# Gate and up of two feed-forward batches by 49 block products in place of 56, and the feed-forward input by way of DRAM

## The chip, the cores and the metric

The kernel runs on one core of one Trainium2 chip. A core has a matrix engine (TensorE, PE in the profile; its weight loads are shown apart as PEld), a vector engine (DVE), a scalar engine (ACT), GpSimd (POOL) and SyncE (SP), which here only issues transfers. Each engine works through its own instructions in their order; semaphores hold one back until another is done. Matrix products write to PSUM (eight banks of 128 x 512 fp32 values), all else lies in SBUF or in DRAM. The metric is the device time of one execution in microseconds, the median of several runs.

## The reference, cut to what matters

Four batches of 512 tokens with 512 channels go through an attention block of the gated delta rule and a gated feed-forward, each with a modulated layer norm in front and a gate behind. What the change touches is the feed-forward:

```python
def _L0_ffn_ref(x, w_gate, w_up, w_down):
    gate = jnp.einsum('bsd,hd->bsh', x, w_gate)
    up = jnp.einsum('bsd,hd->bsh', x, w_up)
    gated = jax.nn.silu(gate) * up
    return jnp.einsum('bsh,dh->bsd', gated, w_down)
...
h = _layernorm(x, axis=-1) * (1 + cb) + sb
x = x + gb * _L0_ffn_ref(h, L0_ffn_w_gate, L0_ffn_w_up, L0_ffn_w_down)
```

Here s is 512, d is 512 and h is 2048; all is fp32.

## The kernel before

The kernel is written with tile pools, and a scheduler of the framework sets the order on each engine: it takes the program's order as a priority and moves instructions forward where it expects an engine to be free. So work of a later stage fills gaps in an earlier one. The stages stand in this order: projections and convolutions of batch 0, its delta rule, projections of the others, and then feed-forward and delta rule in turn: `triangles(2)`, `feed_forward(0)`, `delta_rule(2)`, `triangles(3)`, `feed_forward(1)`, `delta_rule(3)`, `feed_forward(2)`, `feed_forward(3)`.

`delta_rule(b)` goes through four chunks of 128 tokens. `operands` (L609) prepares, `scan` (L682) is the sequential part (products pf at L695 and pm at L704 with copies between them, eight steps per batch), `finish` and `project` normalise, multiply by the output weights (pwo, L745) and write the residual `xmid` to DRAM, and `turned` (L759) transposes the normed result (pxn, L762) into the SBUF tile `hf[b]`, of four channel blocks by 512 tokens. `pending` holds steps that the next scan steps pop.

`feed_forward(b)` takes `hf[b]` and goes over the 16 hidden blocks of 128 in pairs (`for i in range(0, NF, 2)`). For each pair `two_blocks` makes gate and then up: a product of 2 x 2 blocks by Strassen's scheme in Winograd's form, seven products of 256 x 256 x 256 in place of eight. Each of them is two fp32 matrix products 128 x 128 by 128 x 256. The sums of the weights were made once, early, by `weight_sums` and lie in DRAM as `wsum` (seven blocks for each pair); the sums of the input (`hs`, L833 to L836) are made once per batch. The results are added up by ACT copies and DVE additions from PSUM (L965 to L974). Silu (L989) and the product of gate and up (L990) finish a hidden tile `hid`.

Four hidden blocks are a quarter. Down works by quarters: `down` as plain products (pd, L847, 128 x 512, 16 of them), with a multiplication by the gate on DVE (L852) and an addition on POOL (L853); or `down_by_seven` (pds, L890, 28 products 128 x 256), with POOL sums of the hidden tile (L865 to L868), weight sums from DRAM (`dsum`, made by POOL in `feed_forward(1)`, L1004 to L1007) and an accumulator in SBUF (ACT L892, DVE L894). By seven go quarters 1 to 3 of batch 2 and 0 to 2 of batch 3; `seven_to_output` turns the accumulator into output in six steps that `some` hands out between products.

PSUM has three banks for `fill` (products of projections and feed-forward), three for `seq` (the delta rule) and two as `scratch`.

Of the kernel before, what the change touches and what calls it, by code (L numbers as in the profile page):

```python
# [33 lines left out]
LATER = 4000  # L34


@with_exitstack
def adaln_block(
# [29 lines left out]
    w1 = ctx.enter_context(tc.tile_pool(name="w1", bufs=1))  # L68
    stage_b = ExitStack()
# [25 lines left out]
    kd, qd, vd, sd, gd, xmid = ([] for _ in range(6))  # L95
    for b in range(B):
        kd.append(dr.tile([P, NP, T], F32, name=f"kd{b}"))
        qd.append(dr.tile([P, NP, T], F32, name=f"qd{b}"))
        vd.append(dr.tile([NT, P, H, DV], F32, name=f"vd{b}"))
        sd.append(dr.tile([NT, DV, H, P], F32, name=f"sd{b}"))  # L100
        gd.append(dr.tile([2, 2, H, NT, C + 1], F32, name=f"gd{b}"))
        xmid.append(dr.tile([T, D], F32, name=f"xmid{b}"))
    wsum = [dr.tile([NF // 2, P, 7, 2, P], F32, name=f"wsum{i}") for i in range(2)]
# [109 lines left out]
    def load_x(b):  # L213
        ts = []
        if b == 2:

            room = w1.tile([P, NT, D], F32, tag="hf", bufs=2, name=f"xt{b}")
        for c in range(NT):
            if b == 2:
                t = room[:, c, :]  # L220
            else:
                t = pa_.tile([P, D], F32, tag="xt", bufs=4, name=f"xt{b}_{c}")
            (act if b else sp).dma_start(t, x[b, c * P : (c + 1) * P, :])
            ts.append(t)
        return ts
# [298 lines left out]
    ex, at, td, ttd, hf = {}, {}, {}, {}, {}  # L524

    def triangles(b):
# [9 lines left out]
        kp = w1.tile([P, NP, T], F32, tag="kp", bufs=1, name=f"kp{b}")  # L536
# [50 lines left out]
        pm = w1.tile([n, S, S], F32, tag="pm", name=f"pm_{b}")  # L587
        sp.dma_start(pm, ad)
        t = w1.tile([n, S, S], F32, tag="ti", name=f"ti_{b}")
        tmp = w1.tile([n, S * S // 4], F32, tag="tip", name=f"tip_{b}")  # L590
# [168 lines left out]
    def turned(b, c, xn):  # L759
        pt = seq(f"pxn{b}_{c}")  # L760
        for k in range(KD):
            pe.transpose(pt[:, k * P : (k + 1) * P], xn[:, k * P : (k + 1) * P], ident)  # L762
        for k in range(KD):
            act.activation(
                hf[b][:, k, c * P : (c + 1) * P], pt[:, k * P : (k + 1) * P], AF.Identity,
                bias=mod_t[:, 2, k, b : b + 1], scale=mod_t[:, 3, k, b : b + 1],
            )

    def delta_rule(b):
        ga = w1.tile([P, D], F32, tag="ga", name=f"ga{b}")  # L770
        sp.dma_start(ga, gate_d[0, b].partition_broadcast(P))
        hf[b] = w1.tile([P, KD, T], F32, tag="hf", bufs=2, name=f"hf{b}")
        st = operands(b, 0)
        for c in range(NT):
            nxt = operands(b, c + 1) if c + 1 < NT else None
            o = scan(b, c, st, nxt)
            finish(b, c, o, ga)
            st = nxt
# [35 lines left out]
    def feed_forward(b):  # L814
        nonlocal pd_

        own = pd_ if b == B - 1 else pc_
        gb = own.tile([P, D], F32, tag="gb", bufs=1, name=f"gb{b}")
        sp.dma_start(gb, gate_d[1, b].partition_broadcast(P))
        xm = []  # L820
        for c in range(NT):
            t = own.tile([P, D], F32, tag="xm", bufs=NT, name=f"xm{b}_{c}")
            sp.dma_start(t, xmid[b][c * P : (c + 1) * P, :])
            xm.append(t)
        ht = hf[b]
# [4 lines left out]
        if more is None:  # L830
            more = own.tile([P, 3, 2, TH], F32, tag="hs", bufs=1, name=f"hs{b}")
# [6 lines left out]
        tdn, acc, left = {}, {}, {}  # L838

        fast = {2: [1, 2, 3], 3: [0, 1, 2]}.get(b, [])  # L840
# [15 lines left out]

        def left_factors(q, j):

            hid = hids[q, j]
            a11, a12, a21, a22 = (  # L860
                hid[:, k, i * TH : (i + 1) * TH] for i in range(2) for k in range(2)
            )
            t = pd_.tile([P, 3, TH], F32, tag="sd", bufs=4, name=f"sd{b}_{q}_{j}")
            s1, s2, s4 = (t[:, k] for k in range(3))
            pool.tensor_add(s1, a21, a22)  # L865
            pool.tensor_sub(s2, s1, a11)
            pool.tensor_sub(a21, a11, a21)
            pool.tensor_sub(s4, a12, s2)  # L868
            left[q, j] = a11, a12, a22, a21, s1, s2, s4

        def down_by_seven(q):


            sums = {}
            for j in range(2):
                a11, a12, a22, a21, s1, s2, s4 = left[q, j]
                wd = wdn[q, j].rearrange("p j (h d) -> p j h d", h=2)
                d1, d2, d4, d3 = (tdn[q, j][:, k] for k in range(4))
                sums[j] = [
                    (a11, wd[:, 0, 0]), (a12, wd[:, 1, 0]), (s2, d2), (s1, d1), (a21, d3),  # L880
                    (s4, wd[:, 1, 1]), (a22, d4),
                ]
            if q == fast[0]:
                acc[0] = pd_.tile([P, 7, 2, 2 * P], F32, tag="acc", bufs=1, name=f"acc{b}")
            for k in range(7):
                o = fill(f"pds{b}_{q}_{k}").rearrange("p (c d) -> p c d", c=2)
                for c in range(2):
                    for j in range(2):
                        l, r = sums[j][k]
                        pe.matmul(o[:, c], l[:, c * P : (c + 1) * P], r, start=j == 0, stop=j == 1)  # L890
                if q == fast[0]:
                    act.copy(acc[0][:, k], o)  # L892
                else:
                    vec.tensor_add(acc[0][:, k], o, acc[0][:, k])  # L894

        def quarter(q):
            if q not in fast:
                return down(q)
            down_by_seven(q)
            if q == fast[-1]:  # L900
                ending.append(seven_to_output())

        def seven_to_output():

            p1, p2, p6, p5, p7, p3, p4 = (acc[0][:, k] for k in range(7))

            def add_to(tokens, k, v):
                ds = slice(k * TH, (k + 1) * TH)
                vec.tensor_tensor(v, v, gb[:, None, ds].broadcast_to([P, 2, TH]), ALU.mult)
                for c in range(2):  # L910
                    pool.tensor_add(xm[tokens + c][:, ds], xm[tokens + c][:, ds], v[:, c])

            vec.tensor_add(p6, p6, p1)
            vec.tensor_add(p1, p1, p2)
            yield
            vec.tensor_add(p7, p7, p6)
            add_to(0, 0, p1)
            yield
            vec.tensor_add(p2, p6, p5)
            vec.tensor_add(p2, p2, p3)  # L920
            yield
            vec.tensor_add(p4, p4, p7)
            add_to(0, 1, p2)
            yield
            vec.tensor_add(p5, p5, p7)
            add_to(2, 0, p4)
            yield
            add_to(2, 1, p5)
            if fast[-1] == NQ - 1:
                for i in range(NT):  # L930
                    sp.dma_start(out[b, i * P : (i + 1) * P, :], xm[i])

        def some(n):
            while ending and n:
                n -= 1
                if next(ending[0], 1):
                    ending.clear()
# [9 lines left out]
        def two_blocks(o, n, src, i):  # L947
# [6 lines left out]
            def product(l, r):  # L954
                count[0] += 1
                if count[0] % 2 == 0:
                    some(1)
                o = half(n)
                for k in range(2):
                    pe.matmul(o, l[:, k], r[:, k], start=k == 0, stop=k == 1)  # L960
                return o
# [14 lines left out]
        for i in range(0, NF, 2):  # L976
# [3 lines left out]
            wd = own.tile([P, 2, D], F32, tag="fwd", bufs=2, name=f"wdn{b}_{i}")  # L980
# [11 lines left out]
            if i == (0 if b == B - 1 else 2):  # L992
                complete()
                if b == 2:
                    stage_b.close()
                    pd_ = ctx.enter_context(
                        tc.tile_pool(name="pd", bufs=2, side="right", reuse_waits="tile")
                    )
            if b == 1:
# [9 lines left out]
            if q in fast:  # L1009
                tdn[q, j] = pd_.tile([P, 4, 2 * P], F32, tag="td", bufs=4, name=f"td{b}_{q}_{j}")  # L1010
                sp.dma_start(tdn[q, j], dsum[i // 2])
                left_factors(q, j)
            if j == 0 and q > 0:
                quarter(q - 1)
        if b == 2:
            pending.append(lambda: quarter(NQ - 1))
        else:
            some(9)
            quarter(NQ - 1)


    pd_ = None
    ending, count = [], [0]
# [38 lines left out]
    pc_ = ctx.enter_context(tc.tile_pool(name="pc", bufs=2, reuse_waits="tile"))  # L1062
# [11 lines left out]
    feed_forward(2)  # L1074
    feed_forward(3)
# [45 lines left out]
```

## Time and profile before

| | us |
|---|---|
| median of 3 runs | 1312.97 (1311.42 to 1314.52) |
| profiled execution, first to last instruction | 1315.2 |
| stretch of the feed-forward of batches 2 and 3 (after the last transposes of batch 3) | from 1043.3 on |
| one quarter in that stretch (1058.86 to 1095.84) | 36.98 |

The profiled execution gives no time but its span, which is 2.2 us above the median of the runs. A row of the profile's groups has the source line, engine, operation, tiles (written from read), form and count; then the busy time and the mean duration of one in ns; then how long the engine was idle just before them and who ended that. An fp32 matrix product shows as two PE records, each with a weight load. In the chain that ended last each piece has its start, its length and the number of instructions.

### The profile page before, as it was taken

To read this page: it belongs to the slowest core of one execution; us is meant where nothing else is said; L and a number is where in the kernel's file an instruction comes from. 1 tells how busy PE (TensorE), PEld (TensorE's weight loads), DVE (VectorE), ACT (ScalarE), POOL (GpSimd) and SP (SyncE) were. 2 spreads that over 40 slices of the span, in tenths; PEclk is the share of its full clock that TensorE was granted. 3 is DMA by queue.
4 is the path that set the end of the run, shared out by engine and by line. 5 is a ranking of instruction groups with operands and counts; after the bars stand their busy time and mean duration, and the time that the engine had idled before them with its cause. 6 is when DMAs were issued, how large, how long until landed. Compare 5 with 4: busy or idle time off the path is not lost.

```text
span 1315.2 us, 18413 instructions
## 1 busy us (share of the span) xinstructions
PE 1234.9 (94%) x6752; PEld 807.1 (61%) x6752; DVE 733.7 (56%) x1574; ACT 383.5 (29%) x740; POOL 290.8 (22%) x357
## 2 busy tenths in 40 slices
PE   6799898999889998999999999799999999999998
PEld 3345355554344565767757666666666578888884
DVE  3665865656188255784445558543555543563564
ACT  2633355554142354211103332101134312112110
POOL 4100214533210012030023121233111221131113
PEclk9799898999899999999999999899999999999999
DMA  7579667667874537664436555544632555444431
GB/s 209 138 203 288 186 173 209 172 212 249 255 205 126 144 98 176 199 202 139 134 113 189 124 126 165 161 130 150 193 85 70 174 186 175 146 152 152 140 114 62
DMA packets 217945, 214.57 MB, mean 163 GB/s; under 512 B 95608, under 2 KB 164216, under 8 KB 217856
## 3 DMA queue, kind: packets, MB, share of 16 engines
q1 hardware_dynamic: 194976, 176.58, 46.4%
q10 hardware_dynamic: 19360, 17.93, 4.2%
q0 software_dynamic: 3520, 18.89, 3.8%
q8 instruction: 54, 0.88, 0.3%
q14 instruction: 35, 0.29, 0.1%
HBM read 159.23 MB, written 50.97 MB: 160 GB/s over the span
## 4 chain that ended last, share of the span: by engine, by line
PE 64%; DVE 14%; DMA 11%; POOL 5%; issue 3%; ACT 2%; SPq 1%; POOLq 0%; DVEq 0%; ACTq 0%
PE phg L960 14%; PE phu L960 11%; PE pd L847 9%; PE pwo L745 5%; PE pds L890 4%; PE pp_v L424 3%; PE pp_g L424 3%; PE pm L704 2%; DVE ti L602 2%; PE scratch L631 2%; DMA wsum<-wsg 2%; DVE tip L598 2%; DMA wsum<-wsu 2%; PE pp_q L424 1%; PE pp_k L424 1%
## 5 line engine op out<-in xcount | busy, mean ns | idle before, releaser
L847 PE MATMUL pd<-wdn,hid 128*128 128x512 f32 x320 | 140.6, 592 | 0.0
L960 PE MATMUL phg<-hf,wg 128*128 128x256 f32 x512 | 138.4, 387 | 1.8 <-DMA wg<-wsum 1.8
L960 PE MATMUL phg<-hs,wg 128*128 128x256 f32 x384 | 103.6, 390 | 5.9 <-DVE hid L967 5.8
L960 PEld LDWEIGHTS phg<-hf,wg 128*128 128x128 f32 x512 | 95.9, 192 | 20.7 <-issue 6.3
L960 PE MATMUL phu<-hf,wu 128*128 128x256 f32 x384 | 101.1, 388 | 2.2 <-DMA wu<-wsum 2.0
L847 PEld LDWEIGHTS pd<-wdn,hid 128*128 128x128 f32 x320 | 60.7, 190 | 68.1 <-issue 63.6
L960 PE MATMUL phu<-hs,wu 128*128 128x256 f32 x384 | 95.6, 382 | 2.5 <-DVE up L973 2.5
L424 PE MATMUL pp_g<-ht,wg 128*128 128x512 f32 x192 | 91.6, 617 | 5.7 <-DMA wg<-in_w_g_dram 4.6
L853 POOL TENSOR_TENSOR xm<-xm,tmpf 128x512 f32<-128x512 f32 x40 | 50.9, 1273 | 206.8 <-DVE tmpf L852 206.8
L424 PE MATMUL pp_v<-ht,wv 128*128 128x512 f32 x192 | 89.3, 609 | 3.5 <-DVE v L503 2.3
L745 PE MATMUL pwo<-wo,ot 128*128 128x512 f32 x192 | 91.8, 608 | 0.0
L965 ACT COPY hid<-phg 128x256 f32<-128x256 f32 x32 | 11.9, 372 | 247.9 <-PE phg L960 247.9
L960 PEld LDWEIGHTS phg<-hs,wg 128*128 128x128 f32 x384 | 71.5, 193 | 20.4 <-DVE hid L967 8.3
L960 PEld LDWEIGHTS phu<-hs,wu 128*128 128x128 f32 x384 | 71.9, 191 | 19.2 <-DVE up L973 7.1
L960 PEld LDWEIGHTS phu<-hf,wu 128*128 128x128 f32 x384 | 71.7, 192 | 15.5 <-issue 3.1
L424 PEld LDWEIGHTS pp_g<-ht,wg 128*128 128x128 f32 x192 | 35.1, 195 | 43.0 <-issue 41.8
L852 DVE TENSOR_TENSOR tmpf<-pd,gb 128x512 f32<-128x512 f32 x40 | 27.5, 689 | 59.4 <-PE pd L847 44.7
L424 PEld LDWEIGHTS pp_v<-ht,wv 128*128 128x128 f32 x192 | 35.2, 193 | 41.5 <-issue 38.5
L989 ACT ACTIVATE hid<-hid 128x1024 f32<-128x1024 f32 x32 | 33.8, 1057 | 86.2 <-DVE hid L973 70.0
L434 DVE SCALAR_TENSOR_TENSOR acc_v<-pp_v,conv_v,acc_v 128x511 f32<-128x511 f32 (+2 forms) x72 | 53.4, 743 | 9.8 <-ACT acc_v L432 8.8
L704 PE MATMUL pm<-r,l 128*128 128x128 f32 x384 | 53.8, 285 | 1.0 <-ACT r L700 0.9
L704 PEld LDWEIGHTS pm<-r,l 128*128 128x128 f32 x384 | 48.2, 194 | 8.9 <-ACT r L700 4.7
(244 smaller groups left out, 2060.1 us busy)
## 6 DMA issues: line engine op xcount, KB each, us to landing
wdn<-in_w_down_t_dram SPq DMA_DIRECT2D x32, 512.0 KB, 4.3
wg<-wsum SPq DMA_DIRECT2D x32, 512.0 KB, 3.8
wu<-wsum SPq DMA_DIRECT2D x32, 512.0 KB, 3.6
wg<-wsum SPq DMA_DIRECT2D x32, 384.0 KB, 4.4
wu<-wsum SPq DMA_DIRECT2D x32, 384.0 KB, 4.3
wsum<-wsg POOLq DMA_DIRECT2D x8, 896.0 KB, 4.3
wsum<-wsu POOLq DMA_DIRECT2D x8, 896.0 KB, 4.6
vd<-v SPq DMA_DIRECT2D x24, 256.0 KB, 3.4
```

What stands on the lines that cost most here:

```text
L424: pe.matmul(pp, w[:, k, :], ht[:, k, :], start=(k == 0), stop=(k == KD - 1))
L434: vec.scalar_tensor_tensor(acc[:, i:], pp[:, : T - i], taps[:, col, TAPS - 1 - i : TAPS - i], acc[:, i:], ALU.mult, ALU.add,)
L598: vec.tensor_tensor(v, pm[:, j, j + 1 :, None].broadcast_to([n, m, j]), t[:, j : j + 1, :j].broadcast_to([n, m, j]), ALU.mult,)
L602: vec.tensor_add(t[:, j + 1 :, :j], t[:, j + 1 :, :j], v)
L704: pe.matmul(pm[:, h], l[:, hs.start + h, 2 * par : 2 * par + 2, :], r[:, par, hs.start + h], start=True, stop=True,)
L745: pe.matmul(pw, ot[:, h, :], wo[:, h, :], start=(h == 0), stop=(h == H - 1))
L847: pe.matmul(pd, hids[q, i // 2][:, i % 2, c * P : (c + 1) * P], wdn[q, i // 2][:, i % 2, :], start=(i == 0), stop=(i == NQ - 1),)
L852: vec.tensor_mul(tmp, pd, gb)
L853: pool.tensor_add(xm[c], xm[c], tmp)
L890: pe.matmul(o[:, c], l[:, c * P : (c + 1) * P], r, start=j == 0, stop=j == 1)
L960: pe.matmul(o, l[:, k], r[:, k], start=k == 0, stop=k == 1)
L989: act.activation(hid, hid, AF.Silu)
```

## The change

The feed-forward input goes through DRAM in all batches. `turned` writes each chunk's transposed result to `hd[b]`, and `feed_forward` (now of batches 0 and 1 alone) loads it into a tile of its own. `kp`, `pm`, `ti`, `tip` of `triangles` move to a pool that is closed before the last two batches, and their feed-forward starts with a new pool `pe`. `dsum` is made in `feed_forward(0)`.

Batches 2 and 3 are computed by a new function `tail`. Gate and up of a quarter (four hidden blocks, four channel blocks, four token blocks of 128) are one `two_level` call: the 2 x 2 scheme of seven products, and each of the seven again by seven, so 49 products of 128 x 128 x 128 in place of 56 (28 products of 128 x 128 x 256). The outer weight sums come from `wsum` as before; the inner ones are made by POOL for each call. A call goes in two halves, of 4 and of 3 outer products: each inner product is a group of 4 or 3 matrix products into one bank. Three banks serve a half: partial sums are left in PSUM, the next group is added to them there, and ACT or DVE takes out the values on the way. The last group of a half (`ending_`) is deferred into the next half, with the DVE additions that unite the outer level. The input sums for both levels are made once per batch (`moving`). Down goes by seven in all quarters but the last of batch 3; `some` is called once per half.

```diff
+TAIL = 2
...
-            room = w1.tile([P, NT, D], F32, tag="hf", bufs=2, name=f"xt{b}")
+            room = pa_.tile([P, NT, D], F32, tag="xr", bufs=1, name=f"xt{b}")
...
+        h = w1.tile([P, KD, P], F32, tag="hf", bufs=2, name=f"hf{b}_{c}")
         for k in range(KD):
             act.activation(
-                hf[b][:, k, c * P : (c + 1) * P], pt[:, k * P : (k + 1) * P], AF.Identity,
+                h[:, k, :], pt[:, k * P : (k + 1) * P], AF.Identity,
                 bias=mod_t[:, 2, k, b : b + 1], scale=mod_t[:, 3, k, b : b + 1],
             )
+        sp.dma_start(hd[b][:, :, c * P : (c + 1) * P], h)
...
-        ht = hf[b]
+        ht = pc_.tile([P, KD, T], F32, tag="hf", bufs=1, name=f"ht{b}")
+        sp.dma_start(ht, hd[b])
...
-            if b == 1:
+            if b == 0:
...
+    def differences(y11, y12, y21, y22, t1, t2, t4):
+        vec.tensor_sub(t1, y12, y11)
+        vec.tensor_sub(t2, y22, t1)
+        vec.tensor_sub(y12, y22, y12)
+        vec.tensor_sub(t4, y21, t2)
+
+    def moving(own, b):
+        y = own.tile([P, 7, 4, P], F32, tag="y", bufs=1, name=f"y{b}")
+        z = own.tile([P, 3, 7, P], F32, tag="z", bufs=1, name=f"z{b}")
+        for m, i, j in ((0, 0, 0), (1, 1, 0), (4, 0, 1), (5, 1, 1)):
+            sp.dma_start(
+                y[:, m].rearrange("p (k t) x -> p k (t x)", k=2),
+                hd[b][:, 2 * i : 2 * i + 2, j * TH : (j + 1) * TH],
+            )
+        differences(y[:, 0], y[:, 4], y[:, 1], y[:, 5], y[:, 3], y[:, 2], y[:, 6])
+        for ms in (slice(0, 4), slice(4, 7)):
+            differences(*(y[:, ms, j] for j in range(4)), *(z[:, j, ms] for j in range(3)))
+        return y, z
+
+    def two_level(o, n, src, q, yz, then):
+        y, z = yz
+        for s, m0, nm in ((0, 0, 4), (1, 4, 3)):
+            ms = slice(m0, m0 + nm)
+            nn = f"{n}_{s}"
+            w = pc_.tile([P, 2, 4, 2, P], F32, tag="fw", bufs=2, name=f"w{nn}")[:, :, :nm]
+            e = pc_.tile([P, 3, 4, P], F32, tag="fe", bufs=2, name=f"e{nn}")[:, :, :nm]
+            for a in range(2):
+                sp.dma_start(w[:, a], src[2 * q + a][:, ms])
+            x11, x12, x21, x22 = (w[:, a, :, k] for a in range(2) for k in range(2))
+            s1, s2, s4 = (e[:, j] for j in range(3))
+            pool.tensor_add(s1, x21, x22)          # L968
+            pool.tensor_sub(s2, s1, x11)           # L969
+            pool.tensor_sub(x21, x11, x21)         # L970
+            pool.tensor_sub(s4, x12, s2)           # L971
...
+            products(ba, x11, y11, True)
+            act.copy(p1, ba)
+            products(bb, s1, t1, True)
+            act.copy(p5, bb)
+            settle()
+            some(1)
+            products(ba, s2, t2, False)
+            act.copy(u2, ba)
+            bc = view(seq(f"pc{nn}"))
+            products(bc, x12, y21, True)
+            vec.tensor_add(c11, bc, p1)            # L1006
+            products(bb, s4, y22, False)
+            vec.tensor_add(c12, bb, u2)            # L1008
+            products(ba, x21, t3, False)
+            vec.tensor_add(c22, ba, p5)            # L1010
+
+            def ending_(...):
+                products(ba, x22, t4, False)
+                act.copy(c21, ba)
+                v = [o[:, :, j] for j in range(4)]
+                if s == 0:
+                    vec.tensor_add(v[1], v[1], v[0])   # L1017
+                    vec.tensor_add(v[2], v[2], v[0])
+                    vec.tensor_add(v[0], v[2], v[3])
+                else:
+                    r = [part[:, :, j] for j in range(3)]
+                    vec.tensor_add(v[2], v[2], r[0])   # L1022
+                    vec.tensor_add(v[3], v[3], v[2])
+                    vec.tensor_add(v[0], v[0], r[1])
+                    vec.tensor_add(v[2], v[2], r[2])   # L1025
+                    then()
+            left_over.append(ending_)
...
+    def tail(bs):
...
+                h = quarter_of(b, q, yz)           # gate: two_level, then Silu over 128x2048
...
+                if late:
+                    late()                         # down of the quarter before
...
+                two_level(
+                    u, f"u{b}_{q}", wsum[1], q, yz,
+                    lambda u=flat[0], h=flat[1]: vec.tensor_mul(u, u, h),   # L1069, 128x2048
+                )
...
+    def down_of(b, q, u, held, ends):              # by seven (L1135), the last quarter plain (L1100)
...
     delta_rule(3)
-    feed_forward(2)
-    feed_forward(3)
+    stage_c.close()
+    stage_t.close()
+    pc_ = ctx.enter_context(tc.tile_pool(name="pe", bufs=2, reuse_waits="tile"))
+    tail(list(range(TAIL, B)))
```

`products(bank_, l, r, first)` issues one matrix product per outer block (L991), the first with `start` set where `first` is true.

## The prediction

> **What bounds the kernel now.** I read the page's busy table first, then the chain that ended last, then the stretch of the last two batches in windows, then single rows. The first lines say that the matrix engine is the kernel:
>
> ```profile
> span 1315.2 us, 18413 instructions
> PE 1234.9 (94%) x6752; PEld 807.1 (61%) x6752; DVE 733.7 (56%) x1574; ACT 383.5 (29%) x740; POOL 290.8 (22%) x357
> ```
>
> The windows cut out two quarters (four hidden blocks of gate and up, plus one down product by seven) of batch 2. PE is busy over 99% of them at the full clock; DVE and POOL are far from it:
>
> ```profile
> core 0: us, PE busy (x) PEld busy (x) DVE busy (x) ACT busy (x) POOL busy (x), PEclk, DMA share, GB/s
> 1058.86:1095.84 36.98, 36.85 (x170) 31.46 (x169) 15.00 (x31) 9.67 (x17) 7.17 (x9) 1.00 0.40 132
> 1095.84:1132.80 36.96, 36.72 (x169) 31.45 (x169) 18.33 (x36) 5.46 (x11) 5.93 (x8) 1.00 0.48 158
> ```
>
> The chain in order of time gives the price of one record (each fp32 product is two records). Its pieces have no gap in them:
>
> ```profile
> 1049.85 9.01 PE pd L847 x21
> 1058.86 6.04 PE phg L960 x28
> ...
> 1085.91 9.93 PE pds L890 x46
> ```
>
> So 6.04/28 = 0.2157 us for 128x256, 9.93/46 = 0.2159 for the same width in the down products, 9.01/21 = 0.429 for 128x512. A quarter's sum is 112 x 0.2157 + 56 x 0.2159 = 36.25 us against 36.97 measured: 0.7 us of waiting. Saving PE work therefore saves time, as long as nothing else becomes late. Rows for the rest (groups by form; the last column of the POOL and ACT rows is idle time, not cost):
>
> ```profile
> L704 PE MATMUL pm<-r,l 128*128 128x128 f32 x384 | 53.8, 285 | 1.0 <-ACT r L700 0.9
> L853 POOL TENSOR_TENSOR xm<-xm,tmpf 128x512 f32<-128x512 f32 x40 | 50.9, 1273 | 206.8 <-DVE tmpf L852 206.8
> L990 DVE TENSOR_TENSOR hid<-hid,up 128x1024 f32<-128x1024 f32 x32 | 39.9, 1248 | 0.4
> L852 DVE TENSOR_TENSOR tmpf<-pd,gb 128x512 f32<-128x512 f32 x40 | 27.5, 689 | 59.4 <-PE pd L847 44.7 <-POOL xm L853 14.7
> L892 ACT COPY acc<-pds 128x512 f32<-128x512 f32 x14 | 8.2, 586 | 21.6 <-PE pds L890 21.6
> ```
>
> **Step A, the streams: -20.1 us.** Gate and up of two batches are 32 calls of 28 records now: 896 x 0.2157 = 193.3 us. After, 16 calls of 98 records at 128x128 = 1568. In the trace, L704 records (128x128, each with its own weights) start 0.1115 us apart at the median (quartiles 0.111 and 0.112): 174.8 us, 18.5 less. A block product has an eighth less work, but at half the width a record costs 0.517 of the wide one, so 3.4% of these streams is given back. Also one more down product goes by seven: 32 x 0.429 = 13.7 against 56 x 0.2159 = 12.1, 1.6 less. Bounds: no cost at the borders of groups, as in the x28 piece above, is what I take; at worst each of the 7 groups in 32 halves pays one 51 ns semaphore record that PE's sequencer shows in the L960 answer: 224 x 0.051 = +11 us.
>
> **Step B, the new cover: +3.4 us in each of 7 places, +23.5 us.** Today PE reads weight sums that were made once. Now each half (4 or 3 block columns) needs four POOL sums, three or four PSUM evictions by ACT, three by DVE, and then three or four DVE adds over 128x512 (L1017 to L1025), and a DVE product of 128x2048 ends each quarter. By the rows: POOL per quarter 2 x (4 x 1.27 + 4 x 1.0) + 4 x 1.27 = 23 us; DVE 2 x (3 x 0.69 + 3 x 0.53 + 7 x 0.69) + 2.4 + 7 x 0.69 = 24 us; PE 2 x 98 x 0.1115 + 12.1 = 33.9 us. On average all fits under PE, so I walk through the place where it need not: up of one quarter followed directly by gate of the next, in the order in which the changed program's instructions stand on each engine. Time 0 is the first product of up; before it a down product has let both weight buffers and their sums get ready.
> - Up's 46 products in front of gate's first end at 46 x 0.223 + 0.15 = 10.4 (0.15 for the ACT copy of the first bank: 0.29 + 0.09 + 0.59 against 0.89 us of cover).
> - Gate's first weights: the buffer (two deep) is free when the deferred product of up's first half ends at 7.9; a 256 KB load lands after 2.8 us (xr), the second of the pair at about 3.7 (512 KB, wg): 10.9 and 11.7. PE waits 0.45, runs to 11.8.
> - Up's deferred product stands next and needs the DVE sum L1010, which stands behind L1017, L1018, L1006, L1019, L1008 on DVE; the first of these waits for ACT until 8.6. 8.6 + 3 x 0.69 + 2 x 0.53 + 0.53 and gaps = 12.4: PE waits 0.65.
> - Gate's fifth group needs POOL's fourth sum: 11.8 + 4 x 1.27 = 16.9, and PE is there at 15.8: 1.2.
> - Now DVE does four adds and the 128x2048 product for up before it may take gate's sums. Clean they end at 14.05 + 4 x 0.7 + 2.4 = 19.3. But POOL is working then, and DVE rows with both inputs in SBUF grow under it: L909 (128x512) 0.675 alone and 0.875 under POOL, L971 (128x256) 0.43 and 0.87, while L970 with a PSUM input stays at 0.425. I take the 128x512 row, x 1.3: 20.9. The down product in PE's order waits for it (0.7), and the next gate bank is freed two DVE sums later, 22.3, where PE without waits would be at 18.8.
> - The last deferred product again stands behind DVE: 0 to 1.2, taken 0.6.
>
> Together 4.1 us against today's 0.7: +3.4. Bounds: DVE clean leaves 0.45 + 0.65 + 1.2 + 0.1 = 2.4 (+1.7); with x 2 on the adds and x 1.75 on the product (L990's longest is 2.15 us) 6.0 (+5.3). Seven such places (quarters 1 to 3 of batch 2, all four of batch 3): +23.5, from +12 to +37. A gain here is excluded: 0.7 is all there is.
>
> [...]
>
> **Step C, the end: +4.5 us.** The last up quarter is one tile: the copy 0.09 + 0.47, four adds 2.8, product 2.4 and gaps are 6 us in which PE has nothing, then 32 x 0.429 = 13.7 as today. Today the last wait is split: PE stands about 1.5 us between 1283 and 1299 (16.0 less 14.97 busy, and modelled ends). Bounds +2 and +6.
>
> **Step D, the first feed-forward: +4 us.** Its input goes to DRAM and back, 1 MB and four DVE subtractions later, and the changed PE order has no gate product any more in front of the last transposes of batch 1's delta rule (11 products, 22 x 0.2157 = 4.7 us, stand there now, and the profile shows them between 521.99 and 535.2 in waits for POOL and DVE). Bounds 0 and 4.7. For the second feed-forward the load hides under down of the first (13.7 us).
>
> **Step E, the delta rule of batch 3: +3 us.** Batch 2's gate starts after y and z are loaded and built (12 DVE instructions, about 7.7 us), so the PE order puts the last down of batch 1 there and has no foreign product between the second and fourth step of the scan. Foreign work from the first scan step to the last transposes falls from 28.7 to 26.4 us. Batch 1 did this stretch with 20.4 us of it in 95.0 us, batch 3 with 28.7 in 97.2: below some 25 us PE waits for the scan. Bounds 0 and 8. The moved dsum sums (32 x 0.73 us of POOL) go from one feed-forward to another of the same length; POOL idles there three quarters of the time: nothing. The SP queue gets four more stores and loads per batch, all behind work that lands long before: nothing; were an output store to hold up a weight load at the change of batch, 2 us.
>
> **Sum.** -20.1 + 23.5 + 4.5 + 4 + 3 = +14.9 us on the span of 1315.2: 1330.1. The median of the runs is 1312.97, 2.2 under this span, so 1328.
>
> **The rivals.** *Faster.* The four adds and the 2048 product end before PE needs the bank (DVE alone at them, as the rows without POOL show), and only the load and the POOL sum are waited for. Then a place costs 1.2 us, +0.5: -20.1 + 3.5 + 11.5 = -5, 1308. It decides at 1.9 us of waiting per place: below that the change gains. For it speaks DVE's 24 us under 33.9; against it that POOL works 23 of the same 34 us. 17%. *DVE becomes the bound.* If every SBUF-only instruction doubles (12 us per quarter), DVE needs 36 of 33.9 us and each quarter is 36 plus today's 0.7 and the load: 6 to 8 us per place, +45 on average: 1313 + 45 - 20.1 + 11.5 = 1349. 15%. *Narrow records don't hold 0.1115 in short groups:* step A's +11 on top, 1339. 8%. *Everything meets at nothing:* 4%. My forecast of a slower kernel near 1328: 56%.
>
> **How the numbers follow.** The range: low end from B's and C's lower bounds with D and E at 1 us each, -20.1 + 12 + 2 + 2 = -4, widened to the faster rival's lower half, 1304; high end from B's upper bound with the others as taken, -20.1 + 37 + 11.5 = +28, and on towards the DVE rival, 1347. What a measurement can tell from no change is about 0.2%, 2.6 us. Faster by more: 17%, the faster rival less its near misses, plus the tail of the main case. Within: 6%. Slower: 77%.
>
> **What would show it.** Right: a changed profile with L991 records 0.11 us apart inside a group, some 175 us in all; quarters of 37 to 39 us instead of 33.9, with PE waits put down to DVE L1008, L1010 and L1069 and POOL L971; L1017 to L1025 at 0.8 to 1.0 us mean; a hole of 5 to 6 us in front of L1100. Wrong: quarters of 35 us or less, L1069 at 2.4 us, or PE waits that name DMA alone.

## The result, and the profile after

Slower, as forecast, but by 101.6 us and not by 15: 1415.36 us at the median (1411.40 to 1416.23, four runs) against 1313.74 (1311.42 to 1316.38) for the kernel before, a ratio of 1.0766, interval 1.0743 to 1.0789. The forecast was 1328, its range ended at 1347. The profiled execution took 1411.40 us with a span of 1409.7, 94.5 more than the span before.

The head of the page:

```profile
span 1409.7 us, 20205 instructions
PE 1248.8 (89%) x7448; PEld 844.1 (60%) x7448; DVE 843.3 (60%) x1569; ACT 426.8 (30%) x796; POOL 473.2 (34%) x461
```

PE falls from 94% to 89%. DVE has five instructions less and 110 us more of busy time: its instructions have become longer. Two quarters of the tail in windows, cut from one 128x2048 product (L1069) to the next:

```profile
core 0: us, PE busy (x) PEld busy (x) DVE busy (x) ACT busy (x) POOL busy (x), PEclk, DMA share, GB/s
1119.40:1163.20 43.80, 38.74 (x254) 35.71 (x253) 30.36 (x34) 10.36 (x17) 28.42 (x21) 0.93 0.39 133
1163.20:1206.80 43.60, 37.40 (x256) 34.38 (x255) 31.38 (x34) 10.36 (x17) 28.61 (x21) 0.97 0.38 133
```

A quarter takes 43.6 us where it took 36.97 before and where its products alone need 33.9. Neither DVE (31) nor POOL (29) is full. The groups of the tail point to why (busy, mean ns; then idle before):

```profile
L1069 DVE TENSOR_TENSOR up<-up,hid 128x2048 f32<-128x2048 f32 x8 | 23.6, 2952 | 0.3
L969 POOL TENSOR_TENSOR eg<-eg,wg 128x384 f32<-128x384 f32 x7 | 16.7, 2381 | 0.5
L1024 DVE TENSOR_TENSOR hid<-hid,partg 128x512 f32<-128x512 f32 x7 | 12.3, 1752 | 0.0
L971 POOL TENSOR_TENSOR eg<-wg,eg 128x512 f32<-128x512 f32 x7 | 12.0, 1707 | 0.0
```

L1024 has the size of L852's 0.69 us and takes 1.75; L971 has the size of L853's 1.27 and takes 1.71; L969, over 128x384 (1.00 us at its shortest in this run), takes 2.4. PE's longest waits in the tail, and the hole before the last down product:

```profile
PE pbg L991 <- POOL eg L971: 15.4, 8, 2.2
PE pds L1135 <- ACT acc L1137: 8.5, 2, 6.8
PE pag L991 <- DMA wg<-wsum: 7.8, 6, 2.7
PE pag L991 <- DVE partg L1010: 7.3, 6, 1.5
PE pd L1100 <- issue: 5.6, 1, 5.6
```

Now the two engines side by side in one change from up to gate (timelines of DVE and of POOL; start, us):

```profile
1157.47 0.70 DVE L1022 TENSOR_TENSOR up<-up,partu 128x512 f32<-128x512 f32 x1 [2.06 <-ACT partu L1014]
1158.10 1.75 DVE L1024 TENSOR_TENSOR up<-up,partu 128x512 f32<-128x512 f32 x1
1159.77 1.75 DVE L1023 TENSOR_TENSOR up<-up 128x512 f32<-128x512 f32 x1
1161.56 1.63 DVE L1025 TENSOR_TENSOR up<-up,partu 128x512 f32<-128x512 f32 x1
1163.22 2.97 DVE L1069 TENSOR_TENSOR up<-up,hid 128x2048 f32<-128x2048 f32 x1
```

```profile
1157.70 1.60 POOL L969 TENSOR_TENSOR eg<-eg,wg 128x512 f32<-128x512 f32 x1
1159.26 1.72 POOL L970 TENSOR_TENSOR wg<-wg 128x512 f32<-128x512 f32 x1
1160.94 1.71 POOL L971 TENSOR_TENSOR eg<-wg,eg 128x512 f32<-128x512 f32 x1
1162.61 1.44 POOL L968 TENSOR_TENSOR eg<-wg 128x384 f32<-128x384 f32 x1
1164.13 2.93 POOL L969 TENSOR_TENSOR eg<-eg,wg 128x384 f32<-128x384 f32 x1
```

Start plus length gives the ends: L1024 ends 0.55 us after sum L969, sum L970 1.13 us after L1024, L1023 0.54 after L970, and so on. They take turns, one add and one sum every 1.67 us. The last sum begins inside the product and ends 0.87 us after it. Only the first add, which begins as a sum ends, takes its 0.70.

**Where the 94.5 us are.** For each stretch I take the records on PE times their start-to-start median (0.112 us for 128x128, 0.216 for 128x256, 0.429 for 128x512, the small shapes likewise); what is left of the stretch I call waiting. The streams of the whole program fall from 1034.9 to 1015.3 us (-19.6). Waiting before the first scan step goes from 71.6 to 67.3 us (-4.3; in the runs below the first scan step comes at 172 to 179 us, with the change and without, so this is no part of it). From there to the end of the last delta rule it goes from 195.6 to 227.0 (+31.4), in the tail behind it from 13.1 to 100.0 (+86.9). The sum is +94.4.

Some 14 of the tail's 100.0 us are not waiting but slower records. In eight stretches of 3.4 or 6.8 us between 1094 and 1391 us the granted clock is 0.50, and records start 0.213 us (128x128) and 0.427 us (128x256) apart in them. They come upon waits of 6.80, 1.96, 1.96, 1.97, 1.96, 1.96, 2.42 and 5.60 us; behind four others, of 2.18, 2.94, 2.71 and 1.96 us, it stays at 1.00. The tail of the kernel before has no such stretch while products run. One of them beside an undisturbed group of the same size (PE's timeline, then the window):

```profile
1157.68 1.16 PE L991 MATMUL pbg<-z,eg 128*128 128x128 f32 x8
1162.70 2.07 PE L991 MATMUL pbg<-y,eg 128*128 128x128 f32 x8 [1.96 <-POOL eg L971]
```

```profile
core 0: us, PE busy (x), PEclk, DMA share, GB/s
1162.60:1166.00 3.40, 3.30 (x15) 0.50 0.02 5
```

### The profile page after: what moved, and what is told of

Same layout as the page of the kernel before. It is cut to its first block, busy times and chain, and to the rows that moved or that the text cites. A ratio compares the mean times of both kernels' runs of the same rounds, so it can differ in the third digit from the quotient of the medians.

```text
span 1409.7 us, 20205 instructions
## 1 busy us (share of the span) xinstructions
PE 1248.8 (89%) x7448; PEld 844.1 (60%) x7448; DVE 843.3 (60%) x1569; ACT 426.8 (30%) x796; POOL 473.2 (34%) x461
## 4 chain that ended last, share of the span: by engine, by line
PE 53%; DVE 19%; DMA 11%; POOL 8%; issue 5%; ACT 2%; SPq 2%; POOLq 0%; ACTq 0%; DVEq 0%
PE pd L848 7%; PE phg L876 6%; PE phu L876 5%; PE pwo L749 4%; PE pp_v L428 3%; DMA wg<-wsum 3%; PE pp_g L428 2%; PE pag L991 2%; PE pau L991 2%; PE pm L708 2%; PE scratch L635 2%; PE pds L1135 2%; DVE ti L606 2%; DVE tip L602 2%; DMA wsum<-wsu 2%
## 5 line engine op out<-in xcount | busy, mean ns | idle before, releaser
L848 PE MATMUL pd<-wdn,hid 128*128 128x512 f32 x256 | 115.3, 597 | 0.0
L848 PEld LDWEIGHTS pd<-wdn,hid 128*128 128x128 f32 x256 | 47.6, 190 | 50.5 <-issue 48.2
L876 PE MATMUL phg<-ht,wg 128*128 128x256 f32 x256 | 72.0, 400 | 3.8 <-DVE yk L646 2.0
L730 POOL TENSOR_TENSOR osq<-o 128x768 f32<-128x768 f32 x16 | 23.7, 1483 | 108.2 <-ACT o L716 108.2
L438 DVE SCALAR_TENSOR_TENSOR acc_v<-pp_v,conv_v,acc_v 128x509 f32<-128x509 f32 (+2 forms) x72 | 53.3, 743 | 10.8 <-ACT acc_v L436 9.9
L876 PEld LDWEIGHTS phg<-ht,wg 128*128 128x128 f32 x256 | 49.6, 199 | 16.0 <-issue 3.3
L876 PE MATMUL phg<-hs,wg 128*128 128x256 f32 x192 | 52.8, 395 | 6.1 <-DVE hid L883 5.8
L749 PEld LDWEIGHTS pwo<-wo,ot 128*128 128x128 f32 x192 | 35.0, 198 | 32.2 <-issue 29.4
L853 DVE TENSOR_TENSOR tmpf<-pd,gb 128x512 f32<-128x512 f32 x32 | 22.0, 689 | 49.4 <-PE pd L848 46.7
L428 PE MATMUL pp_q<-ht,wq 128*128 128x512 f32 x96 | 51.4, 671 | 0.0
L876 PE MATMUL phu<-ht,wu 128*128 128x256 f32 x192 | 49.1, 381 | 0.4 <-DMA wu<-wsum 0.4
L428 PE MATMUL pp_k<-ht,wk 128*128 128x512 f32 x96 | 45.4, 607 | 3.8 <-DMA wk<-in_w_k_dram 2.6
```

The source lines that it names most:

```text
L428: pe.matmul(pp, w[:, k, :], ht[:, k, :], start=(k == 0), stop=(k == KD - 1))
L438: vec.scalar_tensor_tensor(acc[:, i:], pp[:, : T - i], taps[:, col, TAPS - 1 - i : TAPS - i], acc[:, i:], ALU.mult, ALU.add,)
L749: pe.matmul(pw, ot[:, h, :], wo[:, h, :], start=(h == 0), stop=(h == H - 1))
L848: pe.matmul(pd, hids[q, i // 2][:, i % 2, c * P : (c + 1) * P], wdn[q, i // 2][:, i % 2, :], start=(i == 0), stop=(i == NQ - 1),)
```

## The experiments

Theory S: DVE instructions with all inputs in SBUF and POOL's sums take turns, so each lengthens the other. Theory P: PE waits for POOL's chain of four sums, and DVE's length lies beside it. Theory D: the weight load sets the quarter. Where no interval is given, a time is a single run and stands beside the kernel before on the same chip (one run of 1321.25 us for the first four).

**No weight sums.** In `two_level`:

```diff
-            pool.tensor_add(s1, x21, x22)
-            pool.tensor_sub(s2, s1, x11)
-            pool.tensor_sub(x21, x11, x21)
-            pool.tensor_sub(s4, x12, s2)
+            s1, s2, s4 = x21, x22, x12
```

> Leaves out the four POOL sums of every half's weights (the products read the loaded blocks x21, x22, x12 in their place), everything else as in the changed kernel. Theory S (DVE instructions whose inputs all lie in SBUF and POOL sums hold each other up: 0.69 becomes 1.7 us and 1.27 becomes 1.7 us): L1023 and L1024 fall from 1.65 to 0.7 us, the product from 2.95 to 2.3, a quarter from about 44 to 36 us, the time to 1350 (1335 to 1365). Theory P (PE waits for the chain of four POOL sums, the slow DVE adds lie beside it): the same 1350, so this run alone does not tell S from P. Theory D (the weight load into two buffers sets the quarter): the quarter keeps over 41 us, the time stays above 1395.

1356.11 us, 59 less than the changed kernel. A quarter:

```profile
1141.80:1178.30 36.50, 35.03 (x255) 32.58 (x254) 23.34 (x35) 10.35 (x17) 5.01 (x4) 1.00 0.46 160
```

The same number of DVE instructions takes 23.3 us and not 31, the product 2.29. D falls: the load is unchanged and the quarter is not. It is left with 9.5 us of PE waits for the load of `wg` in the tail.

**Sums made, but unread.**

```diff
+            spare = pc_.tile([P, 4, P], F32, tag="tmpf", bufs=1, name=f"spare{nn}")[:, :nm]
...
-            pool.tensor_sub(x21, x11, x21)
+            pool.tensor_sub(spare, x11, x21)
             pool.tensor_sub(s4, x12, s2)
+            s1, s2, s4 = x21, x22, x12
```

> POOL makes the same four sums, but the products read the loaded blocks and nobody waits for the sums (the third is written to a tile of its own, not in place). Theory S: DVE adds stay at 1.5 to 1.7 us and the product at 2.9, so the waits put down to DVE (L1010, L1139, the gate's banks behind the product) stay; about half of the loss remains: a quarter of 39 to 41 us, 1375 to 1392. Theory P: all of the gain of the run without sums, 1345 to 1360, though DVE is slow. Theory D: above 1395.

1416.18 us: nothing gained, a quarter still 43.7 us. P falls, since no PE wait names POOL any more and the time is the same. My arithmetic for S fell too: not half of the loss stays but all of it. PE now runs ahead until the down product, and there waits for the slow DVE chain, in the longest wait of the tail (L1071 is the 128x2048 product):

```profile
PE pds L1137 <- DVE up L1071: 24.3, 7, 3.6
```

**No outer adds.**

```diff
-                if s == 0:
-                    vec.tensor_add(v[1], v[1], v[0])
...
-                    vec.tensor_add(v[2], v[2], r[2])
-                    then()
+                if s:
+                    then()
```

> Leaves out the outer DVE adds L1017 to L1019 and L1022 to L1025; POOL sums and the 128x2048 product stay. Theory S: the POOL sums go back to 1.27 us outside the product, the DVE waits go, the quarter falls to 37 to 39 us and the time to 1360 to 1375. Theory P: only the lengthened part of the four sums goes (6.3 to 5.1 us), 1 to 2 us a quarter: 1398 to 1408. Theory D: 1405 or more.

1371.29 us, within S's bounds; the quarter is 41.0, above them. The sums are back at 1.26 us, but POOL makes the four sums for the down product (L1109 to L1112) ahead of the gate's now, and PE waits 19.3 us in the tail for the gate's first sum. So the POOL chain has a price of its own once DVE is out of the way. In the changed kernel taking that wait away gained nothing (the run before this one).

**The down sums back in the second feed-forward** (`if b == 1` in place of `if b == 0`).

> The sums of the down weights are made in the second feed-forward again, as before the change, the rest as changed. If moving them costs nothing on the whole (my prediction's term): 1415 within 3, with the first feed-forward some 10 us shorter (first L699 record of batch 2 near 703 us and not 713) and the second one longer by as much. Rival: the move is a loss by itself, through POOL sums beside the DVE instructions of the first feed-forward: 1403 to 1408.

1414.56 us: on the whole nothing, as predicted. But the 10 us in the first feed-forward did not go with them (first L699 record of batch 2 at 712.8 us, 713.0 in the changed kernel): they come from something else, see the runs on the input through DRAM.

**The engines by themselves.** A series of 16 instructions per engine over 128x512 in each stretch:

```diff
+    def sums(n=N, w=D):
+        for _ in range(n):
+            pool.tensor_add(xp[3][:, :w], xp[0][:, :w], xp[1][:, :w])
+    def adds():
+        for _ in range(N):
+            vec.tensor_add(xv[3], xv[0], xv[1])      # from_bank: (xv[3], bank, xv[1]) with bank in PSUM
+    def copies():
+        for _ in range(N):
+            vec.tensor_copy(xv[3], xv[0])            # act_copies: act.copy(xa[1], xa[0])
```

> A kernel of its own that computes nothing of the reference: series of 16 DVE and 16 POOL instructions over 128x512, each alone and then two series started together. Theory S, if the two engines take turns: adds with both inputs in SBUF and POOL sums together last as long as one series after the other (0.6 x 16 + 1.2 x 16 = some 29 us in place of 20), the 128x2048 products the same, while adds with one input in PSUM leave POOL at 1.27 us and stay at 0.6 to 0.7. If instead they only share a bandwidth (my prediction's x 1.3): DVE at 0.9 us and POOL at 1.3 to 1.4. No expectation for one-input copies, for adds that write PSUM and for ACT.

The windows hold, in this order: sums alone; adds and sums; adds from PSUM and sums; one-input copies and sums; ACT copies and sums.

```profile
core 0: us, DVE busy (x) ACT busy (x) POOL busy (x), PEclk, DMA share, GB/s
51.79:73.15 21.36, 0.00 (x0) 0.00 (x0) 20.19 (x16) 1.00 0.00 0
74.31:92.70 18.39, 18.00 (x12) 0.00 (x0) 17.52 (x12) 1.00 0.00 0
114.47:122.41 7.94, 7.57 (x12) 0.00 (x0) 7.55 (x6) 1.00 0.00 1
183.92:203.50 19.58, 19.12 (x14) 0.00 (x0) 18.49 (x15) 1.00 0.00 0
240.71:251.08 10.37, 0.00 (x0) 9.89 (x16) 9.74 (x9) 1.00 0.00 0
```

Alone, sums start 1.340 us apart and adds 0.727 (the same where ACT runs beside them). Together both start 1.667 us apart, twelve of each in the second window: they take turns, in a little less than the sum of both (2.07). The first two adds, which begin before POOL's first sum, take 0.69 us, the others 1.63. With one input in PSUM, adds stay 0.725 apart and sums 1.340. Adds that write PSUM from two SBUF inputs again take turns at 1.667, and one-input copies, 0.42 us alone, go to 1.37 at 1.400 apart. ACT and POOL left each other alone (copies 0.65 us apart and sums 1.34, as alone). The products were not measured under POOL here: the program's order put them ahead of the sums. The lengths in the changed kernel are close to those of the series: trains of adds at 1.75 and 1.63 us (1.63 here), and sums at 1.60 to 1.72 (1.59, the first 1.72).

**Outer adds with one input in PSUM.** Each of the seven adds per call keeps its place and size, but reads a PSUM tile in place of its second input (so the sums of the outer level are left out):

```diff
+                ps_ = scratch[:, 0].rearrange("p a (b c) -> p (a b) c", c=P)
-                    vec.tensor_add(v[1], v[1], v[0])
+                    vec.tensor_add(v[1], ps_, v[0])
```

> The changed kernel with as many instructions on every engine; only the second input of the seven outer DVE adds per call (L1017 to L1025) is a PSUM tile (the numbers added are wrong). In the series run by themselves a DVE add with one input in PSUM and a POOL sum left each other alone. Theory S (both inputs in SBUF is what holds the two engines up): the adds take 0.69 us, POOL sums 1.27 outside the product, a quarter 38 to 41 us, the time 1362 to 1385. Rival (the number of instructions and the order of the waits set the quarter, not where the operands lie): a quarter of 43 us or more, 1405 to 1418.

1378.73 us, 37 less than the changed kernel with the same instructions on every engine. The adds take 0.69 us although POOL is at work beside them, and POOL's 128x512 sums fall to means of 1.27 to 1.34, but for the gate's L971 (mean 1.85: two of seven meet the product and take 3.3, the others 1.27):

```profile
1112.60:1150.50 37.90, 35.37 (x254) 32.99 (x252) 23.49 (x36) 10.38 (x18) 24.60 (x21) 1.00 0.44 154
```

Three of the seven quarters took 37.8 to 37.9 us, the others, the first and the change of batch among them, 41.9 to 43.1. So here where the second input lies decided, not how many instructions wait for each other: S.

**The sums on DVE** (`vec.` for `pool.` in the four sums).

> The changed kernel with the four weight sums of every half made by DVE in place of POOL, so that the engine with more to do gets 10 us more per quarter (16 sums at 0.69 and 0.55) and POOL keeps only the four sums of the down factors. Theory S: the DVE instructions go back to 0.7 us, DVE is busy 34 us of a quarter of 37 to 40 us: 1365 to 1390, faster than the changed kernel. Theory P (DVE as the engine that everything waits for, whatever POOL does): a quarter of 43 us or more, 1405 to 1430.

1365.28 us (1359.42 to 1370.76), ratio to the kernel before 1.0339, interval 1.0302 to 1.0375: some 50 us faster than with the sums on POOL, though the engine with more work got all of it:

```profile
1110.20:1148.90 38.70, 35.39 (x254) 32.76 (x253) 32.24 (x51) 10.34 (x17) 5.81 (x4) 1.00 0.44 150
```

DVE makes 17 instructions more than in the changed kernel's quarter in the same 31 to 32 us.

**No sums, three weight buffers** (`bufs=3` for `fw` on top of the first run).

> The changed kernel without the POOL weight sums, as in the first run, and with three weight buffers in place of two. The wait for the weight load (1.5 us per quarter in that run) goes if two buffers are its cause: a quarter of 35 us in place of 36.6, 1343 to 1348 where the run with two buffers gave 1356. If the load is late for another reason (its place in SP's order): 1353 to 1358.

1335.06 us (before: 1318.12 at the median of seven). The time is below the forecast, but not for the reason given: no PE wait names the load any more, yet the quarter goes from 36.5 to 36.1, not to 35, because the wait moves to the DVE product (6.6 us in seven). Most of the rest of the 21 us lies at the change of batch (41.5 to 37.2), in the last delta rule (106.0 to 101.9) and in the 6.7 us by which this run reached its first scan step earlier. Even without the sums and with loads on time this version of the two-level kernel stays above the kernel before.

**The input through DRAM, alone.** The kernel before, with the hidden tiles stored and loaded again. In the first of two runs the loaded copy shared two buffers with what the delta rule writes:

```diff
+        sp.dma_start(hd[b][:, :, c * P : (c + 1) * P], hf[b][:, :, c * P : (c + 1) * P])
...
-        ht = hf[b]
+        ht = w1.tile([P, KD, T], F32, tag="hf", bufs=2, name=f"ht{b}")
+        sp.dma_start(ht, hd[b])
```

> The kernel before with one part of the change: the feed-forward input is stored to DRAM and loaded again, gate, up and down as before. My prediction's step D: the first feed-forward starts 4 us later (0 to 4.7), the others hide the load: +4 us, ratio 1.000 to 1.004. Rival: each of the four feed-forwards pays for store, load and four subtractions behind them: +12 to +20 us, ratio 1.009 to 1.015.

1347.81 us, ratio 1.0223 (1.0187 to 1.0260). The second feed-forward's load was issued at 743.2 us, behind a store of the running delta rule on SP, and its products began at 758.7 us instead of 692.0: not the change's own case. With a tile of its own, as the change has it (`ht = pc_.tile(...)`, `hf` by token tile):

> The kernel before with one part of the change, the feed-forward input stored by token tile and loaded again into a tile of its own (in the earlier run of this part the loaded copy shared two buffers with what the delta rule writes, and the load of the second feed-forward was issued 51 us late). My prediction's step D, 0 to +5 us: ratio 1.000 to 1.004. The changed kernel's own trace suggests more, +9.6 us up to the end of the last delta rule: if that is this part's price and not that of the two-level products, 1.006 to 1.010.

1344.07 us, ratio 1.0233 (1.0149 to 1.0317): this part alone costs some 30 us, not 4. The first product of the first feed-forward, before and in this run:

```profile
521.99 1.03 PE L960 MATMUL phg<-hf,wg 128*128 128x256 f32 x4
```

```profile
548.72 1.65 PE L963 MATMUL phg<-ht,wg 128*128 128x256 f32 x3 [1.09 <-DMA wg<-wsum]
```

With `act.dma_start` or `pool.dma_start` for the store:

> As the run of the kernel before with the feed-forward input through DRAM (ratio 1.023), but ACT, which writes the tile, issues its store, so that no load of the delta rule stands behind it on SP's queue. If the place on SP is what costs: ratio 1.003 to 1.012. If it is the trip itself (store, load and four subtractions before the first product, and the products that fill the scan of batch 1 coming later): 1.017 to 1.026, with the first product of the first feed-forward still some 25 us later than in the kernel before (522.0 us).

> The same with the store issued by POOL. Place on SP: 1.003 to 1.012, or somewhat more if the store waits behind POOL's sums. The trip itself: 1.017 to 1.026.

By ACT 1332.35 us, ratio 1.0131 (1.0074 to 1.0188); by POOL 1329.24, 1.0109 (1.0046 to 1.0172). Neither theory alone (POOL's time lies in the range of the place on SP, ACT's between the two ranges): off SP, some 13 to 16 us of the 30 seem to come back, though the intervals overlap, and the rest stays, with the first product still late, at 540.7 and 542.1 us. The waiting from the first scan step to the last transposes says the same: 19 us above the kernel before with the store on SP, some 7 and 4 off it. On SP the store waits for ACT, with the delta rule's loads behind it; the SP queue in the scan of batch 1 shows the same line in the changed kernel:

```profile
SPq L773 <- ACT hf L769: 6.1, 2, 3.5
```

PE's written order changed with each of these edits as well (with the store off SP, the norms of the queries move in the first delta rule), so the share of the queue and that of the order are not told apart.

## Why the prediction was right and wrong

**Step A, right.** Streams: -19.6 measured, -20.1 forecast. L991 records start 0.112 us apart at the median, in short groups too, so the rival that they don't falls. At a granted clock of 0.50 they start 0.213 apart, which no step had.

**Step B, the step that failed.** Its walk named the load, POOL's fourth sum and DVE L1010, and PE waits for all three; for the product, which it named too, no PE wait of the changed kernel is put down. The term that was mis-sized is the slowdown of DVE under POOL, x 1.3 from one row. For the product it held (2.29 us alone, 2.97 here). For the second to fourth add of up it measured x 2.4 to 2.5 (0.69 to 1.63 and 1.75) in seven quarters, for the gate's x 1.3 to 2.5, and POOL's sums, which the walk held at 1.27 and 1.0, took 1.7 and, beside the product, up to 3.04. The row misled because L909 met sums of half the size (L911, 128x256). The kernel before had another: L972, an add over 128x256 of 0.42 us, took 0.83 beside such sums in eight places and 1.57 beside POOL's 128x768 instruction L732 (1.5 us). Its length went with that of the POOL instruction. The prediction saw a doubled row (L971), used x 2 for its upper bound alone and took the x 1.3 of L909 for the sum.

The walk also stopped at up to gate. In the other half of each quarter the gate's adds meet the down factors' and up's sums. L1018 takes 1.75 us there, L1010 comes late behind it, and the down product waits for L1139 (from the chain that ended last; start, us):

```profile
1172.02 1.75 DVE hid L1018
...
1174.25 1.21 DVE hid L1019
1175.45 0.48 DVE partg L1010
...
1175.98 0.94 PE pag L991 x6
...
1182.79 0.61 DVE acc L1139
```

A place costs 43.6 - 33.9 = 9.7 us, +9.0 on today's 0.7 and not +3.4, 63 us in seven. The change of batch takes 47.6 us; in the first quarter batch 3's subtractions stand among the gate's adds at up to 1.7 us, and the first down product waits 6.8 us for ACT. In all, the tail's waiting grows by 86.9 where B and C had 28. Without the sums it grows by 27.8, so 59 of the 86.9 go with the sums. That 27.8 is near 28 is chance: it holds 9.5 us of waits for the load, and the input through DRAM alone adds 6.8 to the tail of the kernel before. The slower records at a clock of 0.50, some 14 us by my estimate from their start-to-start times, are within the 86.9; the walk had no term for them, and without the sums they are some 5.

**Rivals.** *DVE becomes the bound* came near in its condition (SBUF-only adds went from 0.69 to 1.63 and 1.75 us, the product from 2.29 to 2.97) and had the wrong price: DVE is busy 31 of 43.6 us, so it isn't full; DVE, POOL and PE stand in one line. *Faster* needed 33.9 + 1.2 us a quarter; even without the sums it is 36.5.

**Step C, right.** The hole before L1100 is 5.6 us (forecast 5 to 6).

**Steps D and E.** Together +7 forecast, +31.4 measured up to the end of the last delta rule. The input through DRAM alone has +19.0 there: D's start of the first feed-forward was named but not its size (542.7 us for 522.0), and "all behind work that lands long before: nothing", said of the stores and loads on SP, was wrong for the store, which stands on SP 6.1 us in the scan of batch 1 until ACT has written its data. The remaining 12.4 are E and whatever else reaches that far. Without the sums 2.5 of them go, with a third weight buffer as well 7.0 more, and 2.9 are left. So they are not mainly B's cause; the two weight buffers seem to weigh more. These are single runs (unread sums alone took 4 us off), so that 2.9 meets the forecast 3 shows little, and E's own cause stays open. The move of the down sums: nothing, as forecast.

## What to carry to other kernels

Before work is moved to an idle POOL, look at what DVE does at that time: here trains of DVE adds that read only SBUF ran in turns with POOL's sums (in the series a pair every 1.667 us, where adds alone start 0.727 and sums alone 1.340 us apart), so count the pair, not each alone. With one input in PSUM both went on as alone (0.725 and 1.340), and even DVE making the sums itself was 50 us faster here. Take a slowdown from a row of trains, not from one of single instructions. Look at the granted clock behind PE's waits too: here it was 0.50 for 3.4 or 6.8 us upon eight of the tail's twelve waits of 1.96 us and more, and the records started 0.213 us apart in place of 0.112. The store on the queue that feeds the scan held the delta rule's loads behind it while it waited for its own data (6.1 us here); how much of the 30 us that is, and how much the later start of the products that fill the scan, is not shown.

## What was not expected of the hardware

One-input DVE copies from SBUF to SBUF are held by POOL's sums nearly as long as two-input adds (0.42 to 1.37 us). A pair in turns (1.667 us) is shorter than its two parts one after the other (2.07). The granted clock of PE, 0.87 in the 43 us up to 1140 us, is no even slowdown: it is 0.50 from 1094.3 to 1101.1 and from 1118.2 to 1125.0 and full between, and the records' distances change with it (0.213 and 0.112 us).
